# Layer 2 of a four-layer network: its inner map kept twice, a row apart, on 64 partitions each, so that one matmul takes two taps of a 3x3 convolution

## The chip, the core and the metric

The kernel runs on one core of a Trainium2 chip. The metric is the device time of one execution, in microseconds (us). The engines are named as the profile names them: PE is the matmul engine (PEld its weight loads), DVE the vector engine, ACT the scalar engine, POOL the GpSimd engine, and SP the engine that only issues DMAs here.

## What is computed

A map of shape (4, 64, 64, 128) goes through four layers, one after the other: a selective scan (layer 0), an attention over all 4096 tokens of an image (layer 1), a block of convolutions (layer 2) and a neighbourhood attention with an MLP (layer 3). Everything is float32. The change is in layer 2 alone:

```python
def _hard_swish(x):
    return x * jnp.clip(x + 3.0, 0.0, 6.0) * (1.0 / 6.0)

def _conv_block(x, w, bn_p, pad):
    return _hard_swish(_bn(_conv(x, w, pad), bn_p))

y = _conv_block(x, cv1_w, cv1_bn, 'VALID')                  # 1x1, 128 to 64 channels
for w1, p1, w2, p2 in ((m0_cv1_w, m0_cv1_bn, m0_cv2_w, m0_cv2_bn),
                       (m1_cv1_w, m1_cv1_bn, m1_cv2_w, m1_cv2_bn)):
    h = _conv_block(y, w1, p1, 'VALID')                     # 1x1, 64 to 64
    h = _conv_block(h, w2, p2, 'SAME')                      # 3x3, 64 to 64
    y = y + h
x1 = _conv(y, cv3_w, 'VALID')                               # 1x1, 64 to 64
x2 = _conv(x, cv2p_w, 'VALID')                              # 1x1, 128 to 64
xc = jnp.concatenate([x1, x2], axis=-1)
xc = _bn(xc, bn_cat)
xc = jnp.where(xc >= 0, xc, 0.1 * xc)
out = _conv_block(xc, cv4_w, cv4_bn, 'VALID')               # 1x1, 128 to 128
```

`h` after the first of the two blocks is the inner map of the title.

## The kernel before

**The order of the whole.** `network` first makes constants and folded weights (`make_layer2` among them, which writes to scratch in DRAM), then runs the scan of image 0. After that, the scan of image i runs beside `rest` of image i-1, which is the scan's output, layer 1, layer 2 and layer 3's attention of that image; the MLP of layer 3 is done beside the next image's scan output. When the scan of image 3 is over, `rest` of image 3 runs alone, in the mode called `wide`, with all of PSUM to itself. So layer 2 runs four times: three times with four PSUM banks beside a scan, once with eight banks and nothing beside it.

No order is written out by hand. A scheduler takes the instructions by priority (the scan has the lower one and fills in), fixes the order on each engine's queue, and puts in every wait. [...]Tiles of a pool rotate: a new one waits until an old one of that name is free.

**The scan.** For each unit POOL multiplies `dB` (L501), ACT makes `dA` (L507), DVE scans (L509), DVE or POOL multiplies by C (L514, L522), and PE sums over the state with four column tiles of 32 (L555, `py`). The products wait in `hc` buffers until PE has taken them.

**Layer 2.** An image has 64 rows of 64 columns. They are cut into two halves of 34 rows (`HALF`, with two rows in common), one on partitions 0 to 63 and one on 64 to 127, 64 channels each. Rows go in chunks of 7, 7, 7, 7 and 6.

- L966: `cv1`, for each half one matmul into its 64 output partitions of a bank (two column tiles).
- L974: the inner 1x1 convolution of both halves in one 128x128 matmul, whose weights are block diagonal (`w_diag`).
- L247, in `conv3x3`, called from `layer2`: nine matmuls for the nine taps of a chunk, each 128x128 block diagonal, added up in one bank. A quarter of each weight block is a half's taps, the other two quarters are zero.
- `hard_swish` (L954, L955 on ACT, L957 on DVE; with the residual L959 and L960) empties a bank of up to 448 columns.
- L994 and L995: `cv3` and `cv2p` side by side in one bank; L1001 and L1006 the last convolution; L1010 stores the result.

The block-diagonal weights are put together once, at the start, in `make_layer2`: a memset on POOL (L897), eight DMAs (L901), and one DMA to scratch (L905). `layer2` loads them for every image as one tile of 128x20x128.

Of the kernel before, what the change touches and what calls it, by code (L numbers as in the profile page):

```python
# [879 lines left out]
def make_layer2(tc, K, A, D, pool):  # L880

    nc = tc.nc

    def fold(out, raw, rows, width):

        nc.gpsimd.tensor_scalar_add(out[:, 0, :], raw[:, 3, :], 1e-3)
        nc.gpsimd.tensor_tensor(out[:, 0, :], out[:, 0, :], K.mhalf[:rows, :width], ALU.pow)
        nc.vector.tensor_mul(out[:, 0, :], out[:, 0, :], raw[:, 0, :])  # L890
        nc.vector.tensor_mul(out[:, 1, :], out[:, 0, :], raw[:, 2, :])
        nc.vector.tensor_sub(out[:, 1, :], raw[:, 1, :], out[:, 1, :])
        nc.vector.tensor_scalar_mul(out[:, 2, :], out[:, 0, :], 1.0 / 6.0)
        nc.vector.tensor_scalar(out[:, 3, :], out[:, 1, :], 1.0 / 6.0, 0.5, ALU.mult, ALU.add)

    diag = pool.tile([128, 20, 128], F32, name="w2_diag")
    nc.gpsimd.memset(diag, 0.0)  # L897
    t = 0
    for name, taps in (("m0_cv1_w", 1), ("m0_cv2_w", 9), ("m1_cv1_w", 1), ("m1_cv2_w", 9)):
        for i in range(2):  # L900
            nc.sync.dma_start(  # L901
                diag[64 * i : 64 * i + 64, t : t + taps, 64 * i : 64 * i + 64], A[f"L2_conv_{name}"]
            )
# [12 lines left out]
    raw = pool.tile([128, 4, 128], F32, name="w2_raw4")  # L916
    nc.sync.dma_start(raw, A["L2_conv_cv4_bn"].partition_broadcast(128))
    last = pool.tile([128, 4, 128], F32, name="w2_last")
    fold(last, raw, 128, 128)
    cv4 = pool.tile([128, 128], F32, name="w2_cv4")  # L920
    nc.sync.dma_start(cv4, A["L2_conv_cv4_w"])
    nc.vector.tensor_mul(cv4, cv4, last[:, 0, :])
    nc.sync.dma_start(D.w2_cv4, cv4)
    nc.sync.dma_start(D.w2_bias, last[0:1, 1, :])


def layer2(tc, K, A, D, img, xT, wide):
# [4 lines left out]
    with ExitStack() as ctx:  # L932
# [12 lines left out]
        n_tok = HALF * W  # L945
        y = big.tile([128, n_tok], F32, name="l2_y")
        h = big.tile([128, n_tok], F32, name="l2_h")
        chunks = [(r, min(7, HALF - r)) for r in range(0, HALF, 7)]

        def hard_swish(ps, bn, out, add=None):  # L950

# [10 lines left out]
        for r0, n in chunks:  # L962
            ps = psum.tile([128, LC], F32, name="ps")
            for i in range(2):
                src = (r0 + i * (H - HALF)) * W
                nc.tensor.matmul(  # L966
                    ps[64 * i : 64 * i + 64, : n * W], cv1, xT[:, src : src + n * W], start=True, stop=True
                )
            hard_swish(ps[:, : n * W], 0, y[:, r0 * W : (r0 + n) * W])
        for m in range(2):  # L970
            for r0, n in chunks:
                cols = slice(r0 * W, (r0 + n) * W)
                ps = psum.tile([128, LC], F32, name="ps")
                nc.tensor.matmul(ps[:, : n * W], diag[:, 10 * m, :], y[:, cols], start=True, stop=True)  # L974
                hard_swish(ps[:, : n * W], 1 + 2 * m, h[:, cols])
            for r0, n in chunks:
                cols = slice(r0 * W, (r0 + n) * W)
                ps = psum.tile([128, LC], F32, name="ps")
                conv3x3(
                    nc,  # L980
                    ps[:, : n * W].rearrange("p (h w) -> p h w", w=W),
                    lambda t, m=m: diag[:, 10 * m + 1 + t, :],
                    h.rearrange("p (h w) -> p h w", w=W),
                    r0,
                    n,
                    HALF,
                )
                hard_swish(ps[:, : n * W], 2 + 2 * m, y[:, cols], add=y[:, cols])
        for c in range(NCH):
            i = c // (NCH // 2)  # L990
            half = slice(64 * i, 64 * i + 64)
            first = (RC * c - i * (H - HALF)) * W
            ps = psum.tile([128, LC], F32, name="ps")
            nc.tensor.matmul(ps[0:64, :], cv3[half, :], y[half, first : first + LC], start=True, stop=True)  # L994
            nc.tensor.matmul(ps[64:128, :], cv2p, xT[:, span(c)], start=True, stop=True)  # L995
# [644 lines left out]
def network(tc, A, out):  # L1640
    nc = tc.nc
    with ExitStack() as ctx:
# [11 lines left out]
        D.w2_diag, D.w2_norms = scratch("w2_diag", [128, 20, 128]), scratch("w2_norms", [128, len(NORMS2), 4])  # L1654
# [120 lines left out]
```

## Time and profile before

| | us |
|---|---|
| median of three runs | 8895.4 (8887.86 to 8905.56) |
| the profiled execution | 8915.71 |
| its span, first to last instruction | 8914.0 |
| PE busy | 7120.9 (80%) |
| DVE busy | 7132.4 (80%) |
| POOL busy | 7043.5 (79%) |
| ACT busy | 5640.4 (63%) |

Layer 2 begins (first L966) at 3271, 5162, 7085 and 8458 us in the span and takes some 115 to 130 us each time. In the lines of the timeline and of the groups, the first numbers are the start and the duration, then come engine, line of the kernel, operation, what is written and what is read (names without buffer numbers), the tile of PE's array (rows*columns), the shape, how many were merged, and in brackets how long the engine had been idle and what ended the wait. The names are those of the program without layer numbers: `l_h` is the inner map, `l_y` the map `y`, `hs_r` a piece of a hard swish. One float32 matmul stands as two records in the trace.

### The profile page before, as it was taken

To read this page: it belongs to the slowest core of one execution; us is meant where nothing else is said; L and a number is where in the kernel's file an instruction comes from. 1 tells how busy PE (TensorE), PEld (TensorE's weight loads), DVE (VectorE), ACT (ScalarE), POOL (GpSimd) and SP (SyncE) were. 2 spreads that over 40 slices of the span, in tenths; PEclk is the share of its full clock that TensorE was granted. 3 is DMA by queue.
4 is the path that set the end of the run, shared out by engine and by line. 5 is a ranking of instruction groups with operands and counts; after the bars stand their busy time and mean duration, and the time that the engine had idled before them with its cause. 6 is when DMAs were issued, how large, how long until landed. Compare 5 with 4: busy or idle time off the path is not lost. (4 is left out here: it accounts for less than half of the span.)

```text
span 8914.0 us, 101143 instructions
## 1 busy us (share of the span) xinstructions
PE 7120.9 (80%) x30116; PEld 2708.4 (30%) x30116; DVE 7132.4 (80%) x8483; ACT 5640.4 (63%) x11581; POOL 7043.5 (79%) x3064
## 2 busy tenths in 40 slices
PE   5844858687689898887798888777888987888987
PEld 2211313132332233333332233233322332353333
DVE  3888878888899999998899989998999989513433
ACT  5646667676566666666766666667766666454355
POOL 5987899989799998998899989988899989500000
PEclk8856968687799998898899998888899988899989
DMA  5777677777555556665555556565445566320020
GB/s 172 248 236 240 224 249 240 262 242 265 180 175 166 172 174 211 192 215 190 165 174 168 176 183 213 194 213 178 165 165 174 180 204 198 107 69 4 7 80 29
DMA packets 864124, 1581.91 MB, mean 177 GB/s; under 512 B 219701, under 2 KB 344780, under 8 KB 859213
## 3 DMA queue, kind: packets, MB, share of 16 engines
q1 hardware_dynamic: 733261, 1399.17, 47.9%
q10 hardware_dynamic: 130304, 176.19, 5.6%
q8 instruction: 241, 3.95, 0.2%
q14 instruction: 318, 2.61, 0.1%
HBM read 1280.47 MB, written 283.59 MB: 175 GB/s over the span
## 5 line engine op out<-in xcount | busy, mean ns | idle before, releaser
L501 POOL TENSOR_TENSOR dB<-du,b_rows 128x1024 f32<-128x1024 f32 x2048 | 4817.8, 2389 | 553.6 <-DVE hc L509 137.0
L507 ACT ACTIVATE dA<-dt,w_A_log 128x512 f32<-128x512 f32 x4096 | 2785.3, 690 | 487.8 <-DVE hc L509 210.9
L509 DVE TENSOR_TENSOR_SCAN dA<-dA,state,dB 128x512 f32<-128x512 f32 x2128 | 2634.8, 1275 | 242.6 <-POOL dB L501 129.4
L522 POOL TENSOR_TENSOR hc<-hc,c_rows 128x1024 f32<-128x1024 f32 x832 | 1988.6, 2390 | 34.7 <-issue 16.1
L509 DVE TENSOR_TENSOR_SCAN hc<-dA,state,dB 128x512 f32<-128x512 f32 x1456 | 1805.4, 1270 | 218.8 <-ACT dA L507 134.6
L514 DVE TENSOR_TENSOR hc<-dA,c_rows 128x512 f32<-128x512 f32 x2432 | 1568.2, 679 | 76.1 <-PE py L555 61.1
L555 PE MATMUL py<-hc,pick 128*32 128x512 f32 x8192 | 1244.2, 685 | 380.2 <-POOL hc L522 307.3
L516 ACT COPY state<-dA 128x1 f32<-128x1 f32 x2128 | 327.6, 158 | 1348.3 <-DVE hc L514 1339.5
L845 PE MATMUL pa<-e,l_v 128*128 128x512 f32 x2048 | 1069.7, 654 | 21.1 <-ACT e L801 19.9
L797 PE MATMUL pair<-l_g,l_f 32*128 32x512 f32 x2048 | 527.1, 663 | 181.1 <-ACT e L801 139.2
L801 ACT ACTIVATE e<-pair 128x1024 f32<-128x1024 f32 (+1 forms) x448 | 508.2, 1134 | 226.9 <-PE pair L797 219.1
L845 PEld LDWEIGHTS pa<-e,l_v 128*128 128x128 f32 x2048 | 375.5, 200 | 673.9 <-issue 618.1
L555 PEld LDWEIGHTS py<-hc,pick 128*32 128x32 f32 x8192 | 211.5, 116 | 1147.5 <-issue 466.4
L247 PE MATMUL ps<-band,w_conv_diag 128*128 128x504 f32 (+3 forms) x1152 | 502.1, 595 | 7.7 <-ACT delta L397 6.6
L1303 PE MATMUL pair<-table,ident 128*128 128x512 f32 x768 | 398.9, 644 | 97.2 <-ACT e L1313 76.5
L509 DVE TENSOR_TENSOR_SCAN dA<-dA,dB 128x512 f32<-128x512 f32 x304 | 356.8, 1215 | 75.6 <-POOL dB L501 62.3
L328 POOL TENSOR_TENSOR du<-delta,xc 128x1024 f32<-128x1024 f32 x128 | 334.7, 2623 | 57.2 <-ACT delta L397 48.9
L1313 ACT ACTIVATE e<-pair 128x1024 f32<-128x1024 f32 (+1 forms) x224 | 254.7, 1137 | 186.5 <-PE pair L1307 185.9
L201 PE MATMUL ps<-ident,ln_xn 128*128 128x128 f32 x512 | 136.5, 362 | 291.0 <-ACT ln_xn L198 221.6
L219 PE MATMUL ps<-xnT,w_fc_w 128*128 128x512 f32 x512 | 271.6, 666 | 71.6 <-ACT xnT L202 44.6
L247 PEld LDWEIGHTS ps<-band,w_conv_diag 128*128 128x128 f32 x1152 | 221.3, 194 | 288.7 <-issue 259.3
L797 PEld LDWEIGHTS pair<-l_g,l_f 32*128 32x128 f32 x2048 | 139.0, 188 | 537.6 <-ACT e L801 275.0
(274 smaller groups left out, 8551.0 us busy)
## 6 DMA issues: line engine op xcount, KB each, us to landing
b_rows<-bc_dram SPq DMA_DIRECT2D x1024, 256.0 KB
c_rows<-bc_dram SPq DMA_DIRECT2D x1024, 256.0 KB
dt<-delta_dram SPq DMA_DIRECT2D x512, 512.0 KB
du<-du_dram SPq DMA_DIRECT2D x512, 512.0 KB
delta_dram<-delta ACTq DMA_DIRECT2D x128, 512.0 KB
du_dram<-du SPq DMA_DIRECT2D x128, 512.0 KB
table<-biasT_dram SPq DMA_DIRECT2D x72, 512.0 KB
y_first_dram<-y_sum ACTq DMA_DIRECT2D x128, 256.0 KB
```

The costliest lines, as they stand in the source:

```text
L247: mm = nc.tensor.matmul(out[:, r0 - row0 : r1 - row0, c0:c1], lhsT((dy + 1) * 3 + dx + 1), src[:, r0 + dy : r1 + dy, c0 + dx : c1 + dx], s ...
L328: nc.gpsimd.tensor_mul(du.rearrange("p d (a b) -> p d a b", b=H), deltas[b].rearrange("p d (a b) -> p d a b", b=H), tk,)
L501: nc.gpsimd.tensor_mul(dB, dus[pp], mid(bt, 2))
L507: nc.scalar.activation(dA, dts[pp][:, g, :], AF.Exp, scale=S.A[:, k, j, pr, g : g + 1])
L509: nc.vector.tensor_tensor_scan(hg[:, order], dA[:, order], dB[:, g, order], 0.0 if i == 0 else state[:, j, pr, g : g + 1], ALU.mult, ALU.add,)
L514: mm = nc.vector.tensor_mul(hc[:, g, :], dA, ct)
L522: made.append(nc.gpsimd.tensor_mul(hc, hc, mid(ct, 2)))
L555: mm = nc.tensor.matmul(py[0][32 * q : 32 * q + 32, :], S.pick, hcs[q // 2][:, q % 2, :], start=(k == 1 and j == 0), stop=(j == NJS - 1),)
L797: nc.tensor.matmul(ps[:, u, :], f[quad, t // 4, span(t % 4, 128)], g[quad, c, :], start=True, stop=True)
L801: made = nc.scalar.activation(e, ps, AF.Exp)
L845: nc.tensor.matmul(pa, v[:, 8 * q + t, :], es[q], start=(t == 0 and q == 0), stop=(t == 7 and q == 3),)
L1303: nc.tensor.matmul(ps[:, u, :], K.ident, t[:, u, :], start=True, stop=False)
```

## The change

The inner map is no longer kept as two halves on 128 partitions. For each half `i` there are now two copies, one on partitions 0 to 63 and one on 64 to 127, both in `h[:, i]`; the upper copy is one row further on than the lower. `y` gets a row of zeros above and below (34 + 2 rows), `h` has 35 rows for each half.

- The inner 1x1 convolution of a chunk: four matmuls of 64x64 (two halves, two copies) into two banks, one for each half, and two hard swishes where there was one. It runs over 35 rows, five chunks of 7.
- The row outside the map is set to zero in each copy by a memset on POOL, in the first chunk (rows 0, lower copies) and in the last (row 34, upper copies).
- The 3x3 convolution: with all 128 partitions one matmul takes the tap above and the middle tap of a column offset (three matmuls for each half), with partitions 64 to 127 alone the tap below (three more). Each has 64 output columns; the two halves are two column tiles of one bank. That is 12 matmuls of 64 columns a chunk in place of 9 of 128.
- The weights are read straight from the inputs by ten DMAs for each image into `points` and `taps`. The memset, the nine DMAs and the scratch of the block-diagonal weights are gone.

```diff
-    diag = pool.tile([128, 20, 128], F32, name="w2_diag")
-    nc.gpsimd.memset(diag, 0.0)
-    t = 0
-    for name, taps in (("m0_cv1_w", 1), ("m0_cv2_w", 9), ("m1_cv1_w", 1), ("m1_cv2_w", 9)):
-        for i in range(2):
-            nc.sync.dma_start(
-                diag[64 * i : 64 * i + 64, t : t + taps, 64 * i : 64 * i + 64], A[f"L2_conv_{name}"]
-            )
-        t += taps
-    nc.sync.dma_start(D.w2_diag, diag)
...
-        diag = load("diag", [128, 20, 128], D.w2_diag)
+        points = big.tile([128, 2, 64], F32, name="w2_points")
+        taps = big.tile([128, 2, 2, 3, 64], F32, name="w2_taps")
+        for m in range(2):
+            source = A[f"L2_conv_m{m}_cv2_w"].rearrange("i (y x) o -> i y x o", x=3)
+            for i in range(2):
+                half = span(i, 64)
+                nc.sync.dma_start(points[half, m, :], A[f"L2_conv_m{m}_cv1_w"][:, 0, :])
+                nc.sync.dma_start(taps[half, m, 0], source[:, i])
+            nc.sync.dma_start(taps[64:128, m, 1], source[:, 2])
...
-        y = big.tile([128, n_tok], F32, name="l2_y")
-        h = big.tile([128, n_tok], F32, name="l2_h")
+        y = big.tile([128, HALF + 2, W], F32, name="l2_y")
+        h = big.tile([128, 2, HALF + 1, W], F32, name="l2_h")
+        for r in (0, HALF + 1):
+            nc.vector.memset(y[:, r, :], 0.0)
...
         for m in range(2):
+            for r0 in range(0, HALF + 1, 7):
+                sides = [psum.tile([128, LC], F32, name="ps") for i in range(2)]
+                for shift in range(2):
+                    for i, ps in enumerate(sides):
+                        half = span(i, 64)
+                        nc.tensor.matmul(
+                            ps[span(shift, 64), : 7 * W], points[half, m, :],
+                            flat(y[half, r0 + shift : r0 + shift + 7, :]), start=True, stop=True,
+                        )
+                for i, ps in enumerate(sides):
+                    hard_swish(ps[:, : 7 * W], 1 + 2 * m, flat(h[:, i, r0 : r0 + 7, :]))
+                if r0 == 0:
+                    nc.gpsimd.memset(h[0:64, :, 0, :], 0.0)
+                if r0 + 7 == HALF + 1:
+                    nc.gpsimd.memset(h[64:128, :, HALF, :], 0.0)
             for r0, n in chunks:
-                cols = slice(r0 * W, (r0 + n) * W)
                 ps = psum.tile([128, LC], F32, name="ps")
-                nc.tensor.matmul(ps[:, : n * W], diag[:, 10 * m, :], y[:, cols], start=True, stop=True)
-                hard_swish(ps[:, : n * W], 1 + 2 * m, h[:, cols])
-            for r0, n in chunks:
-                cols = slice(r0 * W, (r0 + n) * W)
-                ps = psum.tile([128, LC], F32, name="ps")
-                conv3x3(
...
-                )
-                hard_swish(ps[:, : n * W], 2 + 2 * m, y[:, cols], add=y[:, cols])
+                out = ps[:, : n * W].rearrange("p (h w) -> p h w", w=W)
+                work = [(alone, dx) for alone in range(2) for dx in (0, -1, 1)]
+                for t, (alone, dx) in enumerate(work):
+                    c0, c1 = max(0, -dx), min(W, W - dx)
+                    rows = slice(64, 128) if alone else slice(0, 128)
+                    for i in range(2):
+                        nc.tensor.matmul(
+                            out[span(i, 64), :, c0:c1], taps[rows, m, alone, dx + 1, :],
+                            h[rows, i, r0 + alone : r0 + alone + n, c0 + dx : c1 + dx],
+                            start=(t == 0), stop=(t == len(work) - 1),
+                        )
+                inner = flat(y[:, 1 + r0 : 1 + r0 + n, :])
+                hard_swish(ps[:, : n * W], 2 + 2 * m, inner, add=inner)
```

More of the change, by code (lines that the diff above doesn't have):

```diff
@@ L944, in layer2, with flat @@
         bias = load("bias", [1, 4, 128], D.w2_bias.unsqueeze(1).to_broadcast([1, 4, 128]))
-        n_tok = HALF * W
-        y = big.tile([128, n_tok], F32, name="l2_y")
-        h = big.tile([128, n_tok], F32, name="l2_h")
+        y = big.tile([128, HALF + 2, W], F32, name="l2_y")
+        h = big.tile([128, 2, HALF + 1, W], F32, name="l2_h")
+        for r in (0, HALF + 1):
+            nc.vector.memset(y[:, r, :], 0.0)
         chunks = [(r, min(7, HALF - r)) for r in range(0, HALF, 7)]
+        def flat(rows):
+            return rows.rearrange("p h w -> p (h w)")
         def hard_swish(ps, bn, out, add=None):
@@ L968, in layer2 @@
                 )
-            hard_swish(ps[:, : n * W], 0, y[:, r0 * W : (r0 + n) * W])
+            hard_swish(ps[:, : n * W], 0, flat(y[:, 1 + r0 : 1 + r0 + n, :]))
         for m in range(2):
+            for r0 in range(0, HALF + 1, 7):
[13 more added lines that the diff above has]
+                    nc.gpsimd.memset(h[64:128, :, HALF, :], 0.0)
@@ L971, in layer2 @@
             for r0, n in chunks:
-                cols = slice(r0 * W, (r0 + n) * W)
                 ps = psum.tile([128, LC], F32, name="ps")
-                nc.tensor.matmul(ps[:, : n * W], diag[:, 10 * m, :], y[:, cols], start=True, stop=True)
-                hard_swish(ps[:, : n * W], 1 + 2 * m, h[:, cols])
-            for r0, n in chunks:
-                cols = slice(r0 * W, (r0 + n) * W)
-                ps = psum.tile([128, LC], F32, name="ps")
-                conv3x3(
[L980 to L986, printed above, removed]
-                )
-                hard_swish(ps[:, : n * W], 2 + 2 * m, y[:, cols], add=y[:, cols])
+                out = ps[:, : n * W].rearrange("p (h w) -> p h w", w=W)
@@ L991, in layer2 @@
             half = slice(64 * i, 64 * i + 64)
-            first = (RC * c - i * (H - HALF)) * W
+            first = 1 + RC * c - i * (H - HALF)
             ps = psum.tile([128, LC], F32, name="ps")
-            nc.tensor.matmul(ps[0:64, :], cv3[half, :], y[half, first : first + LC], start=True, stop=True)
+            nc.tensor.matmul(ps[0:64, :], cv3[half, :], flat(y[half, first : first + RC, :]), start=True, stop=True)
             nc.tensor.matmul(ps[64:128, :], cv2p, xT[:, span(c)], start=True, stop=True)
@@ L1653, in network @@
         D.conv_diag = scratch("conv_diag", [128, ND, 9, 128])
-        D.w2_diag, D.w2_norms = scratch("w2_diag", [128, 20, 128]), scratch("w2_norms", [128, len(NORMS2), 4])
+        D.w2_norms = scratch("w2_norms", [128, len(NORMS2), 4])
         D.w2_cv4, D.w2_bias = scratch("w2_cv4", [128, 128]), scratch("w2_bias", [1, 128])
```

## The prediction

> **What bounds the kernel now.** I read the page's busy slices first, then the work by stretches of time, then the timeline around each of the four runs of layer 2, then the waits of POOL and the start of the kernel.
>
> The slices, and two rows of the table by stretches (PE, PEld, DVE, ACT, POOL busy us; then granted clock, DMA share, GB/s). 7070 to 7200 holds layer 2 of image 2, beside the scan of image 3; 8456 to 8578 holds layer 2 of image 3, when the scan is over:
>
> ```profile
> PE   5844858687689898887798888777888987888987
> POOL 5987899989799998998899989988899989500000
> 7070.00:7200.00 130.00, 122.47 (x422) 52.86 (x422) 105.95 (x131) 81.86 (x163) 95.43 (x42) 0.96 0.44 144
> 8456.00:8578.00 122.00, 112.37 (x333) 53.40 (x332) 34.04 (x57) 47.25 (x74) 0.00 (x0) 0.96 0.10 31
> ```
>
> For most of the span POOL is full. In a layer-2 stretch PE is (94% and 92%), and POOL waits for it. The timeline, image 0 then image 3:
>
> ```profile
> 3271.22 3.23 PE L966 MATMUL ps<-xT,w_cv_w 128*64 128x448 f32 x16 [1.00 <-PE py L555]
> 3288.26 9.68 PE L247 MATMUL ps<-l_h,w_diag 128*128 128x448 f32 x18 [1.54 <-DVE l_h L957]
> 3329.44 2.38 POOL L501 TENSOR_TENSOR dB<-du,b_rows 128x1024 f32<-128x1024 f32 x1 [10.75 <-PE ps L974]
> ...
> 8464.10 0.74 ACT L954 ACTIVATE hs_r<-ps,w_norms 128x448 f32<-128x448 f32 x1
> 8465.32 0.75 ACT L954 ACTIVATE hs_r<-ps,w_norms 128x448 f32<-128x448 f32 x1
> 8469.81 32.13 PE L247 MATMUL ps<-l_h,w_diag 128*128 128x448 f32 x90 [0.47 <-DVE l_h L957]
> 8537.41 1.07 PE L994 MATMUL ps<-l_y,w_cv 64*64 64x512 f32 x2
> 8538.41 1.07 PE L995 MATMUL ps<-xT,w_cv2p_w 128*64 128x512 f32 x2
> ```
>
> The reader is to see four things. A matmul is two records: 90 for the 45 of one convolution, back to back, 0.357 us a record, so the convolution is bound by streamed columns alone. L966 already uses two column tiles of 64: 16 records of 448 columns took 3.23 us, 8 slots of 0.375 plus 0.23, so two tiles stream at once. L994 and L995 also have different column tiles, but 64 against 128 rows, and do not overlap: 1.00 us apart for 0.857 us of streaming. And a hard swish costs ACT 1.22 us (8464.10 to 8465.32).
>
> While the convolution runs no scan product gets PE, so POOL runs out of buffers: it idles 10.8, 13.8 and 7.6 us at the end of the first convolution of images 0 to 2 and 15.0, 18.6 and 23.5 us at the second's.
>
> The scan of image 3 ends at about 7700, but image 2's layer 3 runs to 7816: the chain through layers 1 to 3 is the late one, the scan fills gaps. Layer 3's chunks are 75 us apart beside the scan (7312.11 to 7388.00) and about 50 after it (7713 to 7814, two chunks). So scan time saved returns about a third.
>
> The start (SPq rows are DMA issues):
>
> ```profile
> 4.70 3.87 SPq L901 DMA_DIRECT2D w_diag<-in_L_conv_m_cv_w  x6
> 9.67 2.01 SPq L901 DMA_DIRECT2D w_diag<-in_L_conv_m_cv_w  x2
> 20.74 20.82 POOL L889 TENSOR_TENSOR w_last<-w_last,mhalf 128x128 f32<-128x128 f32 x1
> 48.11 0.78 ACT L202 ACTIVATE xnT<-ps,w_ln_b,w_ln_w 128x512 f32<-128x512 f32 x1 [13.73 <-DMA w_ln_w<-in_L_conv_ln_w]
> ```
>
> The eight diagonal loads stand on SP ahead of the load that feeds the 20.82 us power on POOL; SP's stores of that result stand ahead of the LayerNorm weights, for which ACT waits 13.73 us.
>
> **What the Trainium skill says.** "TensorEngine Tiling (Array Packing)", Key Properties: tiles run independently, and changing the tiling mode drains TensorE. The trace agrees on both: L966 overlaps, L994 and L995 lose 0.14 us each. Same page, PSUM Bottleneck: tiling speeds TensorE, not the emptying of PSUM; here that is ACT's 1.22 us. "TensorE: Matmul & The Clock Gate", Part 1: an idle array falls to half clock; between 8459 and 8462, after little work, L966's weight loads come 0.75 us apart and not 0.375.
>
> **The change part by part, layer 2 of image 3 (nothing else running).**
> - Convolution. 9 full matmuls become 6 pairs of column tiles. Per chunk 12 slots of 0.36 us, 4.32; two changes between 128 and 64 rows. Their cost: 0.14 each from L994, at most a slot each (0.36) plus a weight load that can't be fetched ahead (0.14); I take 0.25. 4.8 a chunk, 24.1 for five against 32.1: -8.0 each, -16.0 for both. No trace shows two column tiles on the same 64 rows; if these alone did not overlap, half of the slots double and a chunk costs about 7.0: +2.9 for five.
> - Inner map. One 128x128 matmul a chunk (3.65 us for five) becomes four 64x64 ones, into two banks. L555's four column tiles took 1.06 us for 512 columns; I take 1.0 a chunk, 5 us; serial would be 3 a chunk. Either hides behind ACT, which has two hard swishes a chunk: 2.44 us, ten more per image, 12.2 us of ACT and 6.1 us of DVE (0.61 each).
> - Start. Before, the first convolution began 8.2 us after the first hard swish. Now the eight banks decide: five maps of y and ten of the copies come first, so the sixteenth tile waits for the release of the eighth: 8 x 1.22 + 0.65 = 10.4, +2.2. The memset of the border on POOL (about 0.2 us, as other memsets of the start; POOL is idle) follows the seventh hard swish and is covered by the wait for the bank; uncovered it costs some 0.3 us.
> - Loads. Ten small DMAs for one: SP issues them every 0.47 us, +4.1 us ahead of the norms. The norms landed 5.44 us after issue behind 1.3 MB; a 256 KB load took 2.83. Net +1.5.
> - Between the convolutions. Before 3.65 us of matmuls, no gap. Now the next convolution's bank is that of the third copy: 1.3 for the last convolution's hard swish, 3 x 1.22, 0.65: 5.7, +2.1.
> - Clock. PE is 40% busy in those stretches and may start at half clock: 0 to 3 us, I take 1.
> Sum: -16.0 + 2.2 + 1.5 + 2.1 + 1 = -9.2 us.
>
> **Images 0 to 2, beside the scan.** PSUM has four banks here. At the start the convolution's tile is the sixteenth, so it waits for the twelfth to be freed, against the seventh before (3288.26 is just when the seventh's DVE step ends). Hard swishes here come every 1.5 to 2.2 us (ten from 3273.06 to 3290.22): +6 to +8 us, 7.4 taken, and 1.4 for the loads. Between the convolutions it was 8.6, 7.7 and 6.9 us (3324.15 to 3332.74 for image 0); now eight hard swishes, about 15.5: +7.8. With -16.0 for the convolutions the chain moves by +0.6 us an image: taken as nothing, with 6 us to each side.
> The scan does gain: each convolution is 8 us shorter, which is POOL idling of 7.5 and 8 us an image; DVE gives back 6.1. About +9 an image, 28 in all, a third of it at the end: -9 us.
> Four memsets an image enter POOL's queue, each waiting for DVE. Behind a waiting one stand the scan's products, for which DVE and then PE wait. POOL has 25 to 35 us of slack in these stretches and the first convolution has 9 us before it needs the border: nothing taken, up to 3 us each if the order is bad.
>
> **Start of the kernel.** Eight DMAs (5.9 us of SP) and a 2.2 us memset go. The power on POOL starts earlier by 5.9, and so do the LayerNorm weights: -6 us, 0 at worst if another load comes last.
>
> **Sum.** -9.2 + 0 - 9 - 6 = -24 us on the profiled run's 8915.7 (span 8914.0). That run is 0.2% above the median of 8895.4; scaled, 8871 us. About 0.2% (18 us) can be told from no change.
>
> **Rivals.**
> - PE alone counts. If gaps beside the scan shrink with PE's load, as PE at 94% suggests, each early image gives its 16.0: -48 - 9 - 6, 8832 us. Against it: ACT, which the copies load, ends the waits (DVE l_h, DVE l_y) in the starts.
> - It is given back. Changes of mode at 0.5 us instead of 0.25, twenty an image, cost 5 us more on each of four images, and the forecast's -24 is down to -4 or so: 8892 us. For it: nothing here switches so often between 128 and 64 rows. Against it: L994's 0.14.
> - Slower: the copies' border. The memset writes row 0 of both copies, a stretch with a hole. If the program's wait takes it as one whole, the convolution waits for all fifteen hard swishes, ten between the two. Price: image 3 +9 at each of two places (15 against 8; 10 against 3), beside the scan three more each, +6 twice: +18 + 36 against -24: 8925 us. It decides from the point where more than about half of the second copy must be done before the first tap. No wait in this profile tells which it is, hence its chance; POOL serving the memset late has the same effect.
>
> **How the numbers follow.** Forecast 0.42, PE alone 0.13, given back 0.18, border 0.27. Faster is 0.36 of the forecast and the PE case, 0.49; the same 0.06 and 0.15, 0.21; slower the border and 0.03, 0.30. The forecast's own range is 8845 to 8890 (switches of 0.14 to 0.5, 6 us an image on the chain); with the other cases 8830 to 8930.
>
> **What would show it.** A convolution of image 3 near 24 us (right) or 32 or more (column tiles on 64 rows don't overlap). Its first matmul 10.4 us after the first hard swish (banks) or 19 (border). POOL's waits at the ends of the convolutions down by 7 to 8 us each. The gap between the convolutions beside the scan near 15 us. The power on POOL beginning near 15 us. Wrong would be: a chain beside the scan that moves by more than 6 us an image either way.

## The result, and the profile after

| | before | after |
|---|---|---|
| median | 8892.1 us (8886.6 to 8905.6) | 8864.4 us (8857.0 to 8869.1) |
| ratio | | 0.9962, 95% interval 0.9952 to 0.9972 |
| the profiled execution | 8915.7 us | 8860.9 us |

The change is worth 0.38% (0.28% to 0.48%), some 28 to 34 us. The two profiled executions differ by more, 54.8 us: before's stands 24 us above its median and after's 4 below, and a second profile of before (below) ends 16.5 us sooner. So differences of milestones between the first two profiles carry something that belongs to one execution: 8 us at the beginning of layer 2 of image 0 by the second profile, 27 at the end by the medians.

The busy slices of after, and two stretches in answer to those of before (7033 to 7163 holds layer 2 of image 2, 8414 to 8536 that of image 3; columns as before):

```profile
PE   6845858686788888887798988887899888888987
POOL 6988999989899999998899989998899989300000
7033.00:7163.00 130.00, 110.75 (x530) 31.23 (x526) 127.04 (x156) 95.72 (x183) 119.47 (x56) 0.88 0.48 154
8414.00:8536.00 122.00, 104.84 (x466) 38.59 (x465) 43.31 (x84) 65.87 (x114) 0.79 (x4) 0.90 0.16 53
```

In the stretch beside the scan PE falls from 122.5 to 110.8 us and POOL, which waited for PE, rises from 95.4 to 119.5; VectorE is now the fullest, 127.0 of 130. That is the lead that the forecast promised the scan. Layer 2 of image 3, alone on the chip:

```profile
8422.17 0.72 ACT L956 ACTIVATE hs_r<-ps,w_norms 128x448 f32<-128x448 f32 x1 [8.86 <-DMA w_norms<-w_norms_dram]
8432.75 22.29 PE L996 MATMUL ps<-l_h,w_taps 128*64 128x448 f32 x114 [0.31 <-issue]
8442.39 0.72 ACT L956 ACTIVATE hs_r<-ps,w_norms 128x448 f32<-128x448 f32 x1 [0.55 <-PE ps L996]
8447.15 0.72 ACT L956 ACTIVATE hs_r<-ps,w_norms 128x448 f32<-128x448 f32 x1 [3.45 <-PE ps L996]
8451.91 0.72 ACT L956 ACTIVATE hs_r<-ps,w_norms 128x448 f32<-128x448 f32 x1 [3.45 <-PE ps L996]
8461.69 22.30 PE L996 MATMUL ps<-l_h,w_taps 128*64 128x448 f32 x114 [0.31 <-issue]
```

ACT waits for each chunk of the convolution, so the distance of its rows is the chunk's period: 4.76 us (8447.15 to 8451.91). The convolution's first matmul comes 10.6 us after the first hard swish, and 0.1 us after VectorE has finished the eighth (8432.64). From the first `cv1` to the end of the last convolution it is 68.7 us, against 79.6 before.

Beside the scan the same stage got longer. Each length is from the first `cv1` of the image, from the timeline:

| image | first convolution begins | the two convolutions together | between them | whole stage |
|---|---|---|---|---|
| 0 | 17.0, after 30.5 | 69.0, after 49.6 | 8.4, after 18.7 | 94.4, after 98.8 |
| 1 | 20.8, after 35.4 | 67.6, after 49.2 | 7.6, after 19.7 | 96.0, after 104.3 |
| 2 | 16.6, after 31.7 | 67.1, after 51.2 | 6.6, after 19.8 | 90.4, after 102.7 |

And one thing stands against the forecast at once: `cv1` of image 0, the first instruction that the new layer 2 touches, already comes at 3217.8 us and not at 3271.2. Most of the gain of the pair of profiles is there before layer 2 has run at all.

### The profile page after: what moved, and what is told of

It reads as the page before. It is cut to its first block, busy times and chain, and to the rows that moved or that the text cites. A ratio compares the mean times of both kernels' runs of the same rounds, so it can differ in the third digit from the quotient of the medians.

```text
span 8859.2 us, 102397 instructions
## 1 busy us (share of the span) xinstructions
PE 7107.5 (80%) x30596; PEld 2643.4 (30%) x30596; DVE 7138.3 (81%) x8531; ACT 5683.3 (64%) x11661; POOL 7046.2 (80%) x3079
## 5 line engine op out<-in xcount | busy, mean ns | idle before, releaser
L845 PE MATMUL pa<-e,l_v 128*128 128x512 f32 x2048 | 1056.5, 647 | 19.8 <-ACT e L801 19.7
```

Of the source, the lines that this page charges most:

```text
L845: nc.tensor.matmul(pa, v[:, 8 * q + t, :], es[q], start=(t == 0 and q == 0), stop=(t == 7 and q == 3),)
```

## The experiments

The theory to start from is that of the forecast (A: layer 2 carries the gain, the start some 6 us). Its rival, put up after the result (B): the start carries it, and layer 2 gives nothing or costs. Ratios are to runs of before on the same chip (its medians there lay between 8892 and 8903 us).

### The start and layer 2 apart

`e1_new_layer_old_start` puts the memset, the eight loads and the store back at the start of after; nobody reads them:

```diff
+    diag = pool.tile([128, 20, 128], F32, name="w2_diag")
+    nc.gpsimd.memset(diag, 0.0)
...
+    nc.sync.dma_start(D.w2_diag, diag)
     norms = pool.tile([128, len(NORMS2), 4, 1], F32, name="w2_norms")
```

> The changed layer 2, with the old start: the diagonal weights are put together and stored at the start as before, though nothing reads them. Theory A (layer 2 carries the gain, as the forecast's sum has it): the start is worth some 6 us, so about 8870 us, 22 us under before. Theory B (the gain arises ahead of layer 2, in the start and the order that follows from it; in layer 2 image 3 gains 10 us and images 0 to 2 give it back): 8890 us or more, level with before. In the trace: the first dB near 114 us under both; under B the first conv output of layer 1 (L618) at some 2265 us, under A nearer to 2230.

`e2_old_layer_new_start` takes them out of before's start, and each image's layer 2 puts its diagonal weights together itself:

```diff
-        diag = load("diag", [128, 20, 128], D.w2_diag)
+        diag = big.tile([128, 20, 128], F32, name="w2_diag")
+        nc.vector.memset(diag, 0.0)
...
+                nc.sync.dma_start(
+                    diag[64 * i : 64 * i + 64, at : at + taps, 64 * i : 64 * i + 64], A[f"L2_conv_{name}"]
+                )
```

> The old layer 2, nine taps on the block-diagonal weights, with nothing at the start: each image puts its diagonal weights together itself (a memset on VectorE and 8 loads, beside layer 1's end or the scan). Theory A: about 8886 us, 6 under before, and layer 2 of image 3 takes 80 us again. Theory B: 8855 to 8868 us, the whole gain of the change or more, since images 0 to 2 lose the 4 to 12 us each that the new layer 2 added beside the scan.

| | old layer 2 | new layer 2 |
|---|---|---|
| old start | 1 | 0.9991 (0.9983 to 0.9999) |
| new start | 0.9955 (0.9942 to 0.9969) | 0.9962 (0.9952 to 0.9972) |

`cv1` of image 0 stood at 3269.5 us in e1 and at 3227.3 in e2. The four corners fit B: the new start is worth 0.45%, 40 us, with the old layer 2 and 26 us with the new one; the new layer 2 is worth 8 us with the old start and costs 6 with the new one, taken together no clear difference from nothing. Each corner has an order of its own from layer 2 on, and what that alone can do is shown below. (e2's layer 2 is not quite before's, since each image builds its weights; its stages beside the scan took 91 to 94 us, before's 90 to 96.) In e1 the scan's last `dB` came at 7646 us and not at 7696 (7686 in the second profile of before), 40 to 50 us sooner, and the end 13.7 us sooner than in the first profile and 2.9 later than in the second: the scan's lead is real, and little of it is returned.

### What a change between 128 and 64 rows costs

`e3_all_taps_128_rows` is after, with zero weights below the lone taps, so that all twelve matmuls of a chunk have 128 rows:

```diff
+            nc.vector.memset(taps[0:64, m, 1], 0.0)
             nc.sync.dma_start(taps[64:128, m, 1], source[:, 2])
...
-                rows = slice(64, 128) if alone else slice(0, 128)
+                rows = slice(0, 128)
```

> The changed kernel, with the lone taps on 128 rows as well: the lower half of their weights is zero (a memset on VectorE), so that all 12 matmuls of a chunk have the same shape. If going between 128 and 64 rows costs 0.25 us each time, as the forecast has it: the chunk's period falls from 4.76 us to about 4.3, a convolution in image 3 from 23.2 us to about 21, and image 3 by some 4 us; in all 4 to 15 us less than after. If switching is free and the rest of the 4.76 us is something else: the period stays within 0.1 us, and the time at after's 8864.

The timeline of e3, image 3, the first convolution and the hard swishes of three of its chunks:

```profile
8439.49 21.91 PE L997 MATMUL ps<-l_h,w_taps 128*64 128x448 f32 x120 [0.31 <-issue]
8448.67 0.72 ACT L957 ACTIVATE hs_r<-ps,w_norms 128x448 f32<-128x448 f32 x1
8453.14 0.72 ACT L957 ACTIVATE hs_r<-ps,w_norms 128x448 f32<-128x448 f32 x1 [3.15 <-PE ps L997]
8457.60 0.72 ACT L957 ACTIVATE hs_r<-ps,w_norms 128x448 f32<-128x448 f32 x1 [3.15 <-PE ps L997]
```

The period is 4.46 us against 4.76. Two changes a chunk cost 0.30, 0.15 each: near the 0.14 that the forecast had from L994 and L995, and not the 0.25 that it took. That it is the change and not slower matmuls on 64 rows, the records of after show one by one: within each half of a chunk the pairs begin 0.37 us apart on 64 rows as on 128, and only the first two steps after a change are longer, 0.47 and 0.43 us. The rest of the 4.8 came right because a slot is 0.37 us (4.46 / 12) and not 0.36. The convolution of image 3 got 1.3 us shorter (23.2 to 21.9), its stage 2.4; the whole, at 0.9970 (0.9957 to 0.9982), can't be told from after. The 4 to 15 us expected did not come.

### Banks, or the hand-over from engine to engine

`e4_interleaved` writes the inner map and the convolution in turn, so that a convolution's bank stands behind fewer of the ten inner sides:

```diff
         for m in range(2):
-            for r0 in range(0, HALF + 1, 7):
...
+            inner_map(m, 0)
+            for c, (r0, n) in enumerate(chunks):
+                if c + 1 < len(chunks):
+                    inner_map(m, 7 * (c + 1))
+                convolve(m, r0, n)
```

> The changed kernel, with the inner map and the convolution written in turn: inner chunks 0 and 1, convolution chunk 0, inner chunk 2, convolution chunk 1 and so on, so that a convolution's first bank waits for three pairs of inner sides and not for the ten of the whole map. If banks set the start of the convolution: beside the scan the first convolution of images 0 to 2 comes some 15 us nearer to cv1's start (30 to 35 us in after), their layer 2 gets 5 to 12 us shorter each, image 3 about 4 us, and the time 5 to 25 us under after. If PE's order or power's hold on POOL and VectorE sets it, the sum from cv1 to the last convolution stays within 3 us an image, and the time at after's.

The ratio is 1.0062 (1.0048 to 1.0076): both theories missed it. The first convolution did come 7 to 11 us nearer to `cv1` (23.8, 24.0 and 23.6 us in images 0 to 2, after 30.5 to 35.4), but the stages grew to 158.4, 158.9 and 153.3 us. Two lines of PE in image 3, and two of ACT:

```profile
8528.79 6.61 PE L996 MATMUL ps<-l_h,w_taps 64*64 64x448 f32 x24 [0.92 <-DVE l_h L959]
8536.32 1.75 PE L996 MATMUL ps<-l_h,w_taps 64*64 64x448 f32 x4 [0.92 <-DVE l_h L959]
...
8517.24 0.72 ACT L956 ACTIVATE hs_r<-ps,w_norms 128x448 f32<-128x448 f32 x1 [7.99 <-PE ps L996]
8525.54 0.72 ACT L956 ACTIVATE hs_r<-ps,w_norms 128x448 f32<-128x448 f32 x1 [4.52 <-PE ps L996]
```

With one chunk ahead the convolution needs the very inner chunk that was asked for just before it, so each chunk is a round trip PE, ACT, DVE, PE, and its period is 8.3 us (8517.24 to 8525.54) even with nothing else running. So the experiment changed more than the banks. It was tried again with two ahead, as the last run:

```diff
+            ahead = len(chunks) if wide else 2
+            for c in range(ahead):
+                inner_map(m, 7 * c)
             for c, (r0, n) in enumerate(chunks):
-                if c + 1 < len(chunks):
-                    inner_map(m, 7 * (c + 1))
+                if c + ahead < len(chunks):
+                    inner_map(m, 7 * (c + ahead))
                 convolve(m, r0, n)
```

It has the short start of `h3_short_start` (below) and the taps of e3 as well.

> The new layer 2 for every image with all taps on 128 rows and the short start; beside a scan the inner map and the convolution are written in turn with the inner map two chunks ahead (inner chunks 0 and 1, inner 2, convolution 0, inner 3, convolution 1 and so on), so that a convolution never waits for the chunk just asked for, as it did in the kernel that was written in turn with one ahead; image 3 has the whole inner map first. If banks (ten inner sides through four of them) are what made layer 2 of images 0 to 2 longer: from cv1 to the last convolution 85 to 95 us each (97 to 104 with the whole inner map first, 90 to 98 with the old layer 2), and 8785 to 8800 us in all. If layer 2 beside the scan is held by the sharing of PE, ACT and VectorE instead: 97 to 104 us again, and 8805 to 8825 us. Image 3: 66 us under both.

The stages took 137.2, 133.6 and 134.0 us, and the whole 0.9961 (0.9947 to 0.9974) where the same start with the old layer 2 beside the scan reached 0.9883. Both expectations missed again. The long waits of PE in image 0:

```profile
3199.81 1.55 PE L968 MATMUL ps<-xT,w_cv_w 128*64 128x384 f32 x4 [13.43 <-DVE l_y L959]
3231.22 2.19 PE L977 MATMUL ps<-l_y,w_points 64*64 64x448 f32 x8 [3.77 <-DVE l_h L959]
3265.10 2.19 PE L977 MATMUL ps<-l_y,w_points 64*64 64x448 f32 x8 [7.60 <-DVE l_y L962]
3291.71 2.29 PE L977 MATMUL ps<-l_y,w_points 64*64 64x448 f32 x8 [6.13 <-DVE l_h L959]
```

In these rows PE waits 4 to 13 us for a step of DVE. L968 reads neither `l_y` nor `l_h`, and L977 does not read `l_h`: in the first, second and fourth row it waits for a bank, which that step frees (the third may be either). So b1 did not take the waits for banks away, and it can't decide between its two theories. A whole inner map first is the better order here; what the banks cost apart from DVE's share of the work stays open. What after itself waits for, its own timeline shows, image 0 and then image 1:

```profile
3243.12 0.72 ACT L956 ACTIVATE hs_r<-ps,w_norms 128x448 f32<-128x448 f32 x1 [0.43 <-DVE l_h L959]
3246.64 1.76 PE L978 MATMUL ps<-l_y,w_points 64*64 64x448 f32 x4
3248.33 24.44 PE L996 MATMUL ps<-l_h,w_taps 128*64 128x448 f32 x114
...
5157.66 0.61 DVE L959 SCALAR_TENSOR_TENSOR l_h<-hs_r,ps 128x448 f32<-128x448 f32 x1
5158.37 25.10 PE L996 MATMUL ps<-l_h,w_taps 128*64 128x448 f32 x114 [4.41 <-POOL dB L501]
```

The row at 3243.12 is the twelfth hard swish of the stage; the first was at 3219.65, so they came every 2.13 us, and the convolution followed some 3 us after the twelfth was done. Before, seven came every 1.76 us (3273.06 to 3283.64). Five more hard swishes at 2.13 us, and six at 0.37 us more each, are 12.9 us, about the 13.5 by which this start grew. It fits the forecast's picture of the sixteenth tile waiting for the twelfth, and images 1 and 2 show that wait itself: the row at 5157.66 is the twelfth hard swish's step on DVE, it ends at 5158.27, and PE, idle for 4.41 us, begins at 5158.37. (The bracket names POOL's last `dB`, but 0.1 us after the twelfth step is where the convolution begins in image 2 too, 7078.89 and 7078.99, and in all three images of e1.) In image 0 the twelfth was done at 3245.27, and other matmuls filled the time up to 3248.33. No experiment took the bank away: with all eight banks of PSUM in use beside the scan more of them couldn't be tried.

### Is it the work at the start, its place, or the order that follows?

The scheduler fixes the order of each queue, and PE's queues can be laid side by side, matmul by matmul:

```
first difference on PE's queue, line numbers apart
before                 and e1_new_layer_old_start : matmul 4300 (cv1 of image 0)
e2_old_layer_new_start and after                  : matmul 4284 (cv1 of image 0)
before                 and e2_old_layer_new_start : matmul 73
```

So there are two orders of PE's queue up to layer 2, one for each start. `n1_null_memset` adds a memset of 128x1 to after, as a change without work:

```diff
+    nothing = pool.tile([128, 1], F32, name="w2_nothing")
+    nc.gpsimd.memset(nothing, 0.0)
     norms = pool.tile([128, len(NORMS2), 4, 1], F32, name="w2_norms")
```

> After, with one memset of 128x1 on POOL (0.1 us) at the start, where the diagonal weights' memset stood. It adds no work to speak of, but gives the scheduler another list to order. Theory W (the work at the start costs the 40 us): cv1 of image 0 within 10 us of after's 3218, time 8855 to 8875. Theory O (the 40 us are a matter of the order that the scheduler happened to find): cv1 of image 0 may land anywhere from 3215 to 3275, and the time anywhere from 8855 to 8900.

Theory W by the numbers: 0.9966 (0.9952 to 0.9979), `cv1` at 3224.9. But the order came out the same as after's on every queue, so this was a repeat of after (5 us apart in the medians, 7 at `cv1`) and no new draw.

`n3_prep_behind` is before with the diagonal weights put together at the end of `make_layer2`:

```diff
-    diag = pool.tile([128, 20, 128], F32, name="w2_diag")
-    nc.gpsimd.memset(diag, 0.0)
...
-    nc.sync.dma_start(D.w2_diag, diag)
     norms = pool.tile([128, len(NORMS2), 4, 1], F32, name="w2_norms")
...
     nc.sync.dma_start(D.w2_bias, last[0:1, 1, :])
+    diag = pool.tile([128, 20, 128], F32, name="w2_diag")
+    nc.gpsimd.memset(diag, 0.0)
...
+    nc.sync.dma_start(D.w2_diag, diag)
```

> Before, with the diagonal weights put together behind all else in make_layer2: the same memset, eight loads and store, but on SP's queue the loads of the norms (cv4_bn among them) stand ahead. Theory Q (the place in the queues is what costs): power of 128x128 on POOL starts near 9 us (20.7 in before, 9.0 with the new start), the first dB near 103, cv1 of image 0 near 3230, time about 8858. Theory T (the transfers themselves cost, and the store of 1.28 MB that has to land before the scan's weights may take the memory): the first dB at 110 us or later, cv1 of image 0 within 10 us of before's 3271, time 8885 to 8900.

The timelines of before, after and n3 at the start, in this order (SPq rows are DMA issues):

```profile
43.87 0.36 SPq L915 DMA_DIRECT2D w_norms_dram<-w_norms  x1
45.37 0.33 SPq L166 DMA_DIRECT2D w_ln_w<-in_L_conv_ln_w  x1
49.44 3.75 PE L345 MATMUL ps<-xnT,w_in_proj_w 128*128 128x512 f32 x4 [22.48 <-DMA w_conv_b<-in_L_conv_conv_b]
```

```profile
9.02 20.82 POOL L889 TENSOR_TENSOR w_last<-w_last,mhalf 128x128 f32<-128x128 f32 x1
37.12 0.33 SPq L905 DMA_DIRECT2D w_norms_dram<-w_norms  x1
38.62 0.33 SPq L166 DMA_DIRECT2D w_ln_w<-in_L_conv_ln_w  x1
42.49 3.75 PE L345 MATMUL ps<-xnT,w_in_proj_w 128*128 128x512 f32 x4 [19.88 <-DMA w_conv_b<-in_L_conv_conv_b]
```

```profile
9.00 20.82 POOL L889 TENSOR_TENSOR w_last<-w_last,mhalf 128x128 f32<-128x128 f32 x1
19.41 0.34 SPq L924 DMA_DIRECT2D w_diag_dram<-w_diag  x1
38.95 0.33 SPq L905 DMA_DIRECT2D w_norms_dram<-w_norms  x1
44.50 3.56 PE L345 MATMUL ps<-xnT,w_in_proj_w 128*128 128x512 f32 x4 [18.48 <-DMA w_conv_b<-in_L_conv_conv_b]
```

L345 is the scan's first projection, and it has waited some 20 us for its weights. Those are asked for only when the last store of `make_layer2` has landed, 1.5 us after its issue: the SP queue's own waits name that store ahead of L166. Before it comes the power of 20.82 us. In n3 the memset, the eight loads and the store are all done at the start, and the power begins at 9.00 as in after; the first `dB` is at 104.4 (102.7 in e2), `cv1` of image 0 at 3228.6 (3227.3 in e2), in e2's order of PE's queue. So up to layer 2 theory Q holds: what cost was the place of the eight loads ahead of the one that feeds the power, with the order that came of it, and not their work. The time, 8881.7 us or 0.9975 (0.9965 to 0.9986), isn't Q's 8858 nor e2's: from `cv1` of image 0 to the end n3 takes 22 us more than e2, with before's layer 2 and another order than e2's from matmul 4284 on. Orders differ by that much, and 10 us between two kernels can't be put down to their edits by the whole time alone.

`p3_late_start` and `p4_memset_on_dve` draw further orders with a late start; `before_again` is a second profile of before. The edit of p3, on after, and that of p4, on before:

```diff
     nc.sync.dma_start(D.w2_norms, norms[:, :, :, 0])
+    nc.sync.dma_start(D.w2_late, norms[:, :, :, 0].rearrange("p n k -> p (n k)"))
...
-    nc.gpsimd.memset(diag, 0.0)
+    nc.vector.memset(diag, 0.0)
```

> After, with one more store at the start, which nothing reads: the norms (128x24) element by element into a scratch of their own. The memory of make_layer2's tiles, and with it the scan's weights, is free only when it has landed, so the scan starts later, without any work on diagonal weights, and the scheduler, which sees the store, finds a third order (other than before's and after's from the 73rd matmul on). Theory L (a late start itself grows fourfold): cv1 of image 0 about 4 us later than after's 3218 to 3227 for each us that the first dB is later. Theory O (before's order was a poor one, drawn by chance, and only the lead itself is systematic): cv1 of image 0 later by the delay of the first dB, give or take 15 us for another order.

> Before, with the memset of the diagonal weights on VectorE in place of POOL. Loads, store and the wait of the scan's weights stay, and the first dB stays within some 4 us of before's 112 to 115; the scheduler finds another order (from the 137th matmul on). Theory O (before's order was a poor draw): cv1 of image 0 some 15 to 40 us ahead of before's 3271, 8865 to 8890 us. Theory L (a late start grows): cv1 of image 0 within 12 us of before's, 8890 to 8905 us.

> The kernel before, unchanged, for a second profile: its first one took 8915.7 us, some 20 above the median. If the 40 us ahead of layer 2 are a property of the kernel, cv1 of image 0 comes at 3265 to 3275 us again; if they were of that one execution, at 3240 to 3255.

```profile
37.45 0.43 SPq L906 DMA_DIRECT2D w_late_dram<-w_norms  x1
53.37 0.33 SPq L166 DMA_DIRECT2D w_ln_w<-in_L_conv_ln_w  x1
57.28 3.75 PE L345 MATMUL ps<-xnT,w_in_proj_w 128*128 128x512 f32 x4 [35.06 <-DMA w_conv_b<-in_L_conv_conv_b]
```

In p3 the added store holds the weights back until 53.37, as meant. All orders together, us in the profiled execution:

| order of PE's queue up to layer 2 | L345 begins | first dB | cv1 of image 0 | from the first dB to cv1 |
|---|---|---|---|---|
| before, before_again, e1 | 49.4 to 50.0 | 111.7 to 114.7 | 3262.9 to 3271.2 | 3149.7 to 3157.8 |
| p4 | 52.7 | 116.0 | 3256.5 | 3140.5 |
| p3 | 57.3 | 118.9 | 3265.1 | 3146.1 |
| after, n1, e2, e3, e4, n3, h1 | 42.3 to 44.5 | 101.0 to 104.4 | 3217.8 to 3228.6 | 3116.8 to 3126.0 |
| h3, b1 | 26.7, 26.8 | 91.4, 91.0 | 3179.6, 3181.2 | 3088.2, 3090.2 |

Within one row all executions agree to 11 us at `cv1` (h3 and b1 share their order only up to 2638 us). Neither L nor O holds as it was put. p3's first `dB` is 18 us later than after's; O allowed `cv1` up to 3260, L asked for some 3290, it came at 3265. p4 landed on the upper edge of O's range and ended at 0.9989 (0.9982 to 0.9995), p3 at 0.9975 (0.9965 to 0.9985). Before's order is a poor one by 4 to 17 us (against p3 and p4, which start later still). The rest, some 15 to 30 us between the first `dB` and `cv1`, goes along with the start in these five orders, but each start has an order of its own, and the table can't tell the two apart. The second profile of before gave 3262.9, just below the first of the two ranges expected, so the difference is the kernel's, 36 to 45 us.

Where it grows, the traces show, and it is no steady growth. Count the scan's progress by its `dB` multiplications, 512 an image. Before is behind after by 13.7 us at the first, 23.9 at the 161st, 52.8 at the 261st and 35.0 at the first of image 1 (12.2, 20.6, 48.1 and 26.7 in the second profile). So it loses most between the 161st and the 261st, some 770 to 1180 us into the span. p3, which starts later still, loses 1.2 us there and is 17.9 us behind at the first and 22.1 at the first of image 1. h3's lead of 9.6 us is down to 2.9 at the first of image 1, and yet its `cv1` comes 38 us before after's: that is won after the scan of image 0. The orders lose and win at different places, and no one growth of the lead is common to them. Nor does `cv1` of image 0 settle the end: p3's comes 47 us after after's and its end 14, so from there on the same layer 2 took 33 us less. What in an order makes these differences is not settled. Only n3 against e2 moved the start with the order kept, by 1.7 us at the first `dB`, and `cv1` moved by 1.3: no growth there, but on a distance that is smaller than what two executions differ by.

### Versions that use this

`h1_old_beside_new_alone` has the new start, the old layer 2 where a scan runs, and the new one (with e3's taps) for image 3:

```diff
-        layer2(tc, K, A, D, img, xT, wide)
+        (layer2_alone if wide else layer2_beside)(tc, K, A, D, img, xT, wide)
```

> The new start; images 0 to 2, whose layer 2 runs beside a scan, with the old layer 2 (diagonal weights put together for each image), and image 3, which runs alone, with the new layer 2 and all taps on 128 rows. If the parts add up: 8858 (old layer 2 with the new start) less 9 to 11 us in image 3, so 8846 to 8850. If the new layer 2 was worth something beside the scan as well: 8855 or more.

0.9941 (0.9928 to 0.9955), median 8849.8. Image 3's stage takes 66.1 us against 77.5 in e2; the difference of the ratios is 12 us, as the parts add up.

`h3_short_start` takes the power and the last store off the scan's path:

```diff
-    raw = pool.tile([128, 4, 128], F32, name="w2_raw4")
-    nc.sync.dma_start(raw, A["L2_conv_cv4_bn"].partition_broadcast(128))
...
+    nc.sync.dma_start(raw[:, :, 0], A["L2_conv_cv4_bn"].rearrange("r c -> c r"))
+    last = pool.tile([128, 4, 1], F32, name="w2_last")
+    fold(last, raw, 128, 1)
...
-                with tc.tile_pool(name="mk_w2", bufs=1, side="right") as pool:
-                    make_layer2(tc, K, A, D, pool)
+                make_layer2(tc, K, A, D, scan_ctx.enter_context(tc.tile_pool(name="mk_w2", bufs=1)))
```

> The kernel of h1 with a shorter start: cv4's norm is folded with its channels on the partitions (power of 128x1, about 0.6 us, in place of 128x128 with 20.8 us on POOL; layer 2 multiplies cv4's weights itself), and make_layer2's tiles have memory of their own, so that the scan's weights needn't wait for its last store. The first normalised tokens reach PE at 42.5 us in the runs with the new start, since the scan's weights are asked for at 38.7 us; here at 20 to 25 us, the first dB near 80. If a microsecond at the start is one at the end: 8825 to 8830. If it grows as in the first four runs (12 us at the first dB, 40 at the end): 8790. If the scan is bound by something that the start doesn't move: 8845 to 8850.

```profile
2.18 0.43 SPq L166 DMA_DIRECT2D w_ln_w<-in_L_conv_ln_w  x1
26.69 3.78 PE L345 MATMUL ps<-xnT,w_in_proj_w 128*128 128x512 f32 x4 [0.93 <-ACT xnT L202]
34.67 0.57 POOL L889 TENSOR_TENSOR w_last<-w_last,mhalf 128x1 f32<-128x1 f32 x1
```

The weights are asked for at 2.18 us and L345 waits for its tokens alone. 0.9883 (0.9868 to 0.9898), median 8798.0 us, about 104 us under before and the best of all; the first `dB` came 11 us sooner than h1's (23 were expected) and the end 52, close to the 8790 us expected if the lead grows. But it is again an order of its own: 10.6 of the 11 us are left at the first `dB` of image 1, and `cv1` of image 0 comes 47 us sooner than h1's. How much of the gain is the start and how much the order isn't shown, and the two edits weren't run apart.

## Why the prediction was right in the sum and wrong in its parts

The forecast was 8871 us, 24 less than before; it came out 28 to 34 less. Point by point:

- **Convolution, -8.0 us each: right.** 23.2 us in image 3 against 24.1 forecast, a chunk 4.76 against 4.8. Two column tiles on the same 64 rows do overlap. The switch was taken too dear (0.25, measured 0.15), the slot a little too cheap (0.36, measured 0.37; the forecast's own line of L966 gave 0.375).
- **Image 3, -9.2 us: right**, -10.9. Its start grew by 4.6 us from `cv1` (forecast 2.2 for the banks, 1.5 for the loads and 1 for the clock), the convolutions with 23.2 each gave 17.8, the gap between them grew by 2.3 (forecast 2.1; its own terms, 1.3, 3 x 1.22 and 0.65, make 5.6 and so 2.0). The bank decided: 10.6 us from the first hard swish against 10.4 forecast, just behind the eighth hard swish, and not the 19 of the border's rival, which is refuted here. The page "TensorEngine Tiling (Array Packing)" of the Trainium skill, section PSUM Bottleneck, has the limit that is left: the tiles speed up TensorE and not the emptying of PSUM, and that is ACT's 1.22 us a side.
- **Images 0 to 2, +0.6 us each: mis-sized.** By the table above the convolutions gave 17.9 us on average (16.0 forecast), the start took 14.4 (7.4 + 1.4), and the gap 11.9 (7.8): +8.4 an image, outside the 6 us allowed. The term at fault is the hard swish beside the scan: 1.5 us for each of the five more, from a row of ten that came every 1.5 to 2.2. That row's own mean is 1.9 us (3273.06 to 3290.22, nine steps), which would have given 9.5 and not 7.4; for the gap the forecast did take 1.9. They came every 2.13 in image 0 and delayed the others too. The forecast had named a chain that moves by more than 6 us an image as the sign of being wrong, and this part of it was.
- **The scan's lead, -9 us: mis-sized, in both factors.** POOL's idle time in the 130 us from `cv1` fell from 31.0, 36.4 and 35.9 us to 15.0, 13.2 and 13.7, some 20 an image instead of 9. Yet layer 2 as a whole was worth -8 us with the old start and +6 with the new, against -18 forecast. The lead is there (the last `dB` 40 to 50 us sooner in e1), but the chain of image 2 is the late one, and it had its own longer layer 2 to pay for; that this is where the lead went is argued, not shown.
- **Start, -6 us: right for the scan's first matmul, and far off for what followed.** L345 began 7.0 us sooner. The power itself began 11.7 us sooner and not 5.9, since the new order put the load that feeds it ahead of four loads of norms and a store that had stood before it. L917 in before and L907 in after are that load, L913 and L903 the norms':

```profile
11.79 2.98 SPq L913 DMA_DIRECT2D w_raw<-in_L_conv_m_cv_bn  x4
14.82 0.58 SPq L917 DMA_DIRECT2D w_raw<-in_L_conv_cv_bn  x1
...
4.69 0.58 SPq L907 DMA_DIRECT2D w_raw<-in_L_conv_cv_bn  x1
6.43 2.39 SPq L903 DMA_DIRECT2D w_raw<-in_L_conv_m_cv_bn  x4
```

  The first `dB` came 12 to 14 us sooner: ACT's order parts before it, some 54 us into after. PE's parts at matmul 73, and `cv1` of image 0 came 36 to 53 us sooner, of which the first `dB`'s lead is a quarter to a third. The forecast took the order of the queues as given; that step failed.

Of the rivals, "PE alone" is refuted by the gaps, which grew, and "given back" by the switch, which cost 0.15 us and not 0.5; beside the scan the convolutions' gain was given back all the same, by the hard swishes. The signs that the forecast named were met for the convolution and the bank, exceeded for POOL's waits, and missed for the gap beside the scan (18.7 to 19.8 us, 15 forecast) and for the power (9.02 us, 15 forecast). So a total close to the truth came from two errors of opposite sign, the start with its order 20 to 34 us too small and layer 2 some 10 to 24 too large. That they cancelled is luck.

## What to carry to other kernels

When a change also touches a preparation, run the change and the preparation apart (two kernels, four corners) before believing any sum: here the part meant as tidying, with the order that it brought, was worth 26 to 40 us and the part meant as the gain about nothing. At the start of a kernel ask what the first useful matmul waits for, and follow memory as well as queues: tiles that reuse the memory of a preparation wait for its last store. And where a scheduler fixes the order, look first where two orders part; if it is ahead of the edited code, what differs from there up to that code isn't the edit's own work, and what differs after it is a mixture of both.

## What was not expected of the hardware

- The granted clock of PE fell to half for stretches of 3.4 us also where PE was at work, and not at the same places in runs of the same layer 2. e1 and p3 had one at the beginning of each convolution of image 3, after none; their convolutions took 24.7 to 24.9 us, after's 23.2. The table by stretches for e1, two pieces of 3.4 us at the beginning of the first convolution (the seventh number is the clock):

```profile
8468.40:8471.80 3.40, 3.29 (x10) 1.30 (x12) 1.57 (x4) 3.40 (x7) 0.00 (x0) 0.54 0.02 5
8471.80:8475.20 3.40, 3.40 (x20) 0.96 (x18) 1.57 (x4) 3.40 (x7) 0.00 (x0) 1.00 0.00 0
```

  Ten records against twenty in the same time. The Trainium skill, "TensorE: Matmul & The Clock Gate", Part 1, has the half clock of an idle array; in e1 it costs 1.5 to 1.7 us at each convolution, though the inner map had PE busy for 2.8 of the 3.4 us before. Why it falls there is open.
- A power of 128x128 on POOL took 20.82 us and one of 128x1 0.57: by these two it goes by the columns, some 0.16 us each.
- A store of 128x24 floats element by element took 15.9 us from its issue to the next load that waited for it (37.45 to 53.37 in p3), where the same floats row by row took 1.5 (43.87 to 45.37 in before).
